# Mamba block and mixture of experts on one core: the skip of y and the output projection are issued half a step later, the kept columns are copied ahead of the first tap

## Chip, cores and metric

The kernel runs on one core of a Trainium2 chip, as one program and one launch. The time is device time in microseconds (us), lower is better. The engines are TensorE (PE for its matmuls, PEld for its weight loads), VectorE (DVE), ScalarE (ACT), GpSimd (POOL) and SyncE (SP, which issues most DMAs). Each has one queue and works it off in order.

## The reference, cut to what matters

Four sequences of 1024 tokens with 256 channels go through a Mamba block, a layer norm, a mixture of experts (MoE) and a second layer norm. All arithmetic is in float32.

```
h = x * rsqrt(mean(x*x) + 1e-5) * norm_scale
xs, res = split(h @ w_in)                       # 512 channels each
res = silu(res)
xs = silu(causal_depthwise_conv(xs, 4 taps) + conv_b)
delta, B, C = split(xs @ w_xproj)               # 16, 16 and 16 columns
delta = softplus(delta @ w_dt + b_dt)
state[t] = exp(delta[t] * A) * state[t-1] + (delta[t] * xs[t]) * B[t]   # 16 states a channel
y[t] = sum over states of state[t] * C[t]
out = (y + xs * D) * res                        # the skip is xs * D
x1 = layernorm(x + (x + out @ w_out))           # the sum of residuals: 2x + projection
normed = x1 * rsqrt(mean(x1*x1) + 1e-8) * norm_weight
moe = shared expert + 2 of 8 routed experts (256 -> 1024 -> 256, relu, sigmoid router)
result = layernorm(x1 + (x1 + moe))
```

## The kernel before, in words

**Tiling.** The tokens are cut into 8 chunks of 512: two for each of the four sequences. A tile of channels by tokens is 128 x 2048: four blocks of 128 channels, each with 512 tokens. The second chunk of a sequence needs the last three columns of the first (the halo of the convolution, kept in `halos`) and the last value of each state (kept in `state`).

**The scan loop.** The program's outer loop runs over 128 steps, 8 chunks by 16 states. One step of one state does:

- `over_partitions` (L427): PE spreads the row of B, and later that of C, over all partitions, into PSUM (`pb`).
- `inputs`: ACT copies `pb` to `b` (L439), DVE multiplies three blocks of `xs` by B (L441), POOL the fourth (L446). In the first chunk it is two and two.
- `scan`, for each block: ACT computes `da = exp(delta * A)` into PSUM (L454), of which two tiles exist, and DVE runs the recurrence along the tokens in place in `hs` (L457).
- `outputs`, half a step later: DVE multiplies `hs` by C (L470), POOL adds it to `y` (L471).
- `keep`: ACT copies the last column of the states (L465), in the first chunk of a sequence.

**Work beside the scan** is written as generators, which the loop advances by one `yield` each time it calls `side`. The list `beside` is advanced twice a step (behind the second and the fourth block), so one `yield` there is half a step. The list `ending`, used for the tail of the last chunk but one and of the last, is advanced after every block, a quarter of a step.

- `front(b, c)` prepares the next chunk: norm, projection, first tap of the convolution (ACT, L317) and its halo copy (ACT, L322), the other three taps (DVE, L325), the silus of `res` of the chunk before (L353) and of `xs` (L355), and softplus. There `y` serves as scratch up to `delta += y` (POOL, L411). Then the skip `y = D * xs` is made by four ACT instructions (L414), and `xs *= delta` by POOL (L417). For the first chunk, `alone` in the code, all of this lies ahead of the loop, on other engines in part.
- `tail(b, c)` finishes the chunk before: `y *= res` (POOL, L493), a wait, then in two halves the output projection `po` (PE, L503, 16 matmuls) and `summed = 2x + po` (DVE, L511) with its statistics; then the norm, the transposes for the router, its sigmoid (L568) and the routing (L575 and on), which feeds the MoE. The last chunk's tail multiplies on DVE and has no such wait.
- `moe` is a generator of its own, which `other_work` advances by 0.85 after every block: up (L841), relu on ACT (L850), down (L870), and gathers (SP) and scatters (POOL) of the routed rows. What is left of it runs after the scan.

The wait in the tail counts half steps, or quarters in the last two chunks:

```
def wait(halves, quarters):
    for _ in range(quarters if of in chunks[-2:] else halves):
        yield
```

**Order.** The program's order is not the engines' order: a scheduler moves instructions on each queue by its own estimate of when their inputs come. `tc.keep_in_program_order(ins)` pins an instruction behind the one that the program issued before it on the same engine. Before the change the pinned ones here are the first matmuls of the output projection and the scaling of `hn` in the front.

**Table loads.** ACT needs another table set for silu, for sigmoid, for the logarithm and for the exponential; the compiler puts a load (ACT_TABLE_LOAD) wherever the set changes in the order that the scheduler chose.

Of the kernel before, what the change touches and what calls it, by code (L numbers as in the profile page):

```python
# [10 lines left out]
ALU = mybir.AluOpType  # L11
# [7 lines left out]
K = 4  # L19
# [4 lines left out]
CHUNKS = [(512, 512)] * NSEQ  # L24
# [46 lines left out]
def mamba_moe_kernel(  # L71
# [18 lines left out]
    nc = tc.nc  # L90
# [92 lines left out]
    halos = const.tile([P, 2, KB, K - 1], F32, tag="halo", name="halos")  # L183
# [31 lines left out]
    def stats(src, mv, tiles, name):  # L215

        for t in range(tiles.start, tiles.stop):
            st = small.tile([P, 6], F32, tag="bnst", name=f"bnst_{name}_{t}")
            nc.vector.bn_stats(st, src[:, t, :])  # L219
            nc.vector.bn_aggr(mv[:, t, :], st)  # L220
# [40 lines left out]
    def front(b, c):  # L261
        s = f"{b}_{c}"
        TC, TT = LEN[b, c], LEN[b, c] // P
        x_sb = xs_in[b, c]


        alone = (b, c) == chunks[0]
# [22 lines left out]
        def projected(m):  # L290
            pi = ps_mix.tile([P, TC], F32, tag="mix", name=f"pi_{s}_{m}")
            for k in range(KD):
                nc.tensor.matmul(  # L293
                    pi, lhsT=w_in_sb[:, k, m * P : (m + 1) * P], rhs=hT[:, k, :],
                    start=(k == 0), stop=(k == KD - 1),
                )
            return pi
# [16 lines left out]
        for k in range(KB):  # L314
            pi, xk = projected(k), xs[:, k, :]
            yield
            nc.scalar.activation(  # L317
                xk, pi, AF.Identity,
                bias=chan_sb[:, k, CB : CB + 1], scale=chan_sb[:, k, CW + K - 1 : CW + K],
            )  # L320
            if c + 1 < len(CHUNKS[b]):
                nc.scalar.copy(halos[:, c % 2, k, :], pi[:, TC - (K - 1) :])  # L322
            for back in range(1, K):
                tap = chan_sb[:, k, CW + K - 1 - back : CW + K - back]
                nc.vector.scalar_tensor_tensor(  # L325
                    xk[:, back:], pi[:, 0 : TC - back], tap, xk[:, back:], ALU.mult, ALU.add
                )
            if alone:
                nc.scalar.activation(xk, xk, AF.Silu)
            yield  # L330
# [77 lines left out]
        for blocks in [slice(k, k + 1) for k in range(KB)] if alone else [slice(0, KB)]:  # L408
            db, xb = delta[:, blocks, :], xs[:, blocks, :]
            engine = nc.vector if alone else nc.gpsimd  # L410
            engine.tensor_tensor(db, db, y[:, blocks, :], ALU.add)  # L411
            yield
            for k in range(blocks.start, blocks.stop):
                nc.scalar.activation(  # L414
                    y[:, k, :], xs[:, k, :], AF.Identity, scale=chan_sb[:, k, CD : CD + 1]
                )
            engine.tensor_tensor(xb, xb, db, ALU.mult)  # L417
        scans[b, c] = (xs, delta, y, parts, gate)
        yield
# [54 lines left out]
    def turns(of):  # L474
# [5 lines that stand above are left out]
        return wait  # L480

    def tail(b, c):
        s = f"{b}_{c}"
        TC, TT = LEN[b, c], LEN[b, c] // P
        at = P + b * SEQ + FIRST[b, c]
        own_sums = sums_of[at : at + TC, :]
        wait = turns((b, c))
        x_sb, res, y = xs_in.pop((b, c)), gates.pop((b, c)), scans.pop((b, c))[2]
        if (b, c) == chunks[-1]:
            for k in range(KB):  # L490
                nc.vector.tensor_tensor(y[:, k, :], y[:, k, :], res[:, k, :], ALU.mult)
        else:
            nc.gpsimd.tensor_tensor(y, y, res, ALU.mult)  # L493
            yield from wait(3, 6)

        summed = two.tile([P, TT, D], F32, tag="rowset", name=f"summed_{s}")
        mv = small.tile([P, TT, 2], F32, tag="mv", name=f"mv_{s}")
        for half in range(2):
            po = ps_mix.tile([P, TT // 2, D], F32, tag="mix", name=f"po_{s}_{half}")
            for i in range(TT // 2):  # L500
                t = half * TT // 2 + i
                for k in range(KB):
                    ins = nc.tensor.matmul(  # L503
                        po[:, i, :], lhsT=y[:, k, t * P : (t + 1) * P], rhs=w_out_sb[:, k, :],
                        start=(k == 0), stop=(k == KB - 1),
                    )
                    if i == k == 0:
                        tc.keep_in_program_order(ins)
            yield from wait(1, 2)
            two_of = slice(half * TT // 2, (half + 1) * TT // 2)  # L510
            nc.vector.scalar_tensor_tensor(  # L511
                summed[:, two_of, :], x_sb[:, two_of, :], 2.0, po, ALU.mult, ALU.add
            )
            stats(summed, mv, two_of, s)
            yield from wait(1, 0)
# [504 lines left out]
    for _ in front(*chunks[0]):  # L1020
        pass
# [5 lines left out]
    for i, step in enumerate(order):  # L1027
        b, c, n = step
        place = chunks.index((b, c))
        more = i + 1 < len(order)  # L1030
        for k in range(KB):
            if k == 0 and more and n + 1 < N:
                over_b = over_partitions(order[i + 1], n + 1)
            if k == KB // 2:
                over_c = over_partitions(step, N + n)
                if more and n + 1 == N:
                    over_b = over_partitions(order[i + 1], 0)
            scan(step, hs, [k])
            if k == 0 and late is not None:
                keep(*late[0:2])  # L1040
            if k == KB // 2 - 1:
                if late is not None:
                    outputs(*late)
                    if n == 0:
                        list_of = ending if place + 1 == len(chunks) else beside
                        list_of.append(tail(*chunks[place - 1]))
                if n == 0 and place + 1 < len(chunks):
                    beside.append(front(*chunks[place + 1]))
                if n == 3:
                    beside.append(scans[b, c][4]())  # L1050
                if n == N // 2 and place + 2 < len(chunks):
                    xs_in[chunks[place + 2]] = load_x(*chunks[place + 2])
                side(beside)
            if k == KB - 1:
                late = (step, hs, over_c)
                if more:
                    hs = inputs(order[i + 1], over_b)
                side(beside)
            side(ending)
            other_work(LEN[b, c] / MAXC)  # L1060
    keep(*late[0:2])
    outputs(*late)
    ending.append(tail(*chunks[-1]))
    while ending:
        side(ending)
# [71 lines left out]
```

## Time and profile before

| | before |
|---|---|
| median of 3 runs | 1607.16 us (1602.42 to 1608.75) |
| the profiled execution | 1604.24 us |
| its span | 1602.5 us (1.74 outside it) |
| mean granted clock of TensorE | 0.881 |
| busy PE, DVE, ACT, POOL | 75%, 81%, 67%, 72% |
| table loads on ACT | 56 of 1283 ns |
| copy of one halo (L322) | 152 ns, 16 of them |
| one skip instruction (L414) | 707 ns, 32 of them |
| `delta += y` (L411) and `xs *= delta` (L417) on POOL | 4.5 to 4.7 us, 7 each |
| `y *= res` (L493) on POOL | 4.75 us, 7 |
| one half of the output projection (L503) | 5.5 us |
| `summed` (L511) | 0.67 us, 16 |

In the profile's groups and timeline an instruction is named by its line, engine and operation, then the output and inputs by the names of their tiles. A bracket at the end of a timeline line tells how long the engine stood idle ahead of the instruction, and what ended this. `x4` means that four instructions of a kind followed each other. Rows of waits give the waiting engine, tile and line, what released it, and then the total in us, the number and the longest. Windows give the busy time of PE, PEld, DVE, ACT and POOL with the number of instructions, then the clock, the share of the DMA engines and GB/s.

### The profile page before, as it was taken

Reading aid. Unit: us, or ns where it says so; the run is one execution under the profiler, and the core shown is the slowest. Engines: PE = TensorE matmul, PEld = TensorE weight load, DVE = VectorE, ACT = ScalarE, POOL = GpSimd, SP = SyncE. Lnnn points to the kernel's source line nnn. Section 1 sums busy time; section 2 is a strip of 40 time slices with the busy share of each in tenths; the row PEclk is TensorE's granted clock in tenths of the full one; section 3 lists DMA queues with packets and bytes.
Section 4 is the critical chain, followed back from the end, with each engine's and each line's share of the span. In section 5 each row is a group of like instructions: output and inputs, shape, how many; then the busy total and the mean of one; then the engine's idle time right before and its main releaser. Section 6 shows DMA issues by size and latency. Waiting matters only on the chain. (4 is left out here: it accounts for less than half of the span.)

```text
span 1602.5 us, 19985 instructions
## 1 busy us (share of the span) xinstructions
PE 1205.6 (75%) x6216; PEld 911.2 (57%) x6216; DVE 1294.8 (81%) x1435; ACT 1069.2 (67%) x2353; POOL 1157.8 (72%) x899
## 2 busy tenths in 40 slices
PE   5254156865678698878888888788878888899990
PEld 1111023653256576667566766675657767789990
DVE  4899899979998798989998999899989899420005
ACT  6556647875678677887688678866896766444442
POOL 2577986798669876898779977997699877531223
PEclk9575577988879999999989999899899999999995
DMA  5000000251016663366326642574176538659996
GB/s 146 0 0 0 0 13 14 83 145 43 14 40 181 181 181 82 123 202 187 82 70 200 213 109 67 169 214 115 44 210 177 160 82 255 188 154 324 312 279 217
DMA packets 160272, 211.59 MB, mean 132 GB/s; under 512 B 20617, under 2 KB 138130, under 8 KB 160162
## 3 DMA queue, kind: packets, MB, share of 16 engines
q1 hardware_dynamic: 135954, 181.75, 35.2%
q0 software_dynamic: 17216, 21.57, 7.5%
q10 hardware_dynamic: 6992, 6.95, 1.3%
q8 instruction: 51, 0.84, 0.2%
q14 instruction: 59, 0.48, 0.1%
HBM read 178.97 MB, written 31.27 MB: 131 GB/s over the span
## 5 line engine op out<-in xcount | busy, mean ns | idle before, releaser
L471 POOL TENSOR_TENSOR y<-y,hs 128x2048 f32<-128x2048 f32 x128 | 596.6, 4661 | 80.3 <-DVE hs L470 80.0
L454 ACT ACTIVATE da<-delta,chan_sb 128x512 f32<-128x512 f32 x512 | 353.0, 694 | 197.2 <-DVE hs L457 194.6
L870 PE MATMUL pd<-w,h 128*128 128x256 f32 x1600 | 386.2, 385 | 24.5 <-ACT h L850 11.6
L870 PEld LDWEIGHTS pd<-w,h 128*128 128x128 f32 x1600 | 298.3, 193 | 91.6 <-issue 20.4
L457 DVE TENSOR_TENSOR_SCAN hs<-da,state,hs 128x512 f32<-128x512 f32 x256 | 317.8, 1270 | 26.1 <-ACT da L454 24.9
L457 DVE TENSOR_TENSOR_SCAN hs<-da,hs 128x512 f32<-128x512 f32 x256 | 302.2, 1209 | 26.1 <-ACT da L454 25.5
L841 PEld LDWEIGHTS pu<-xT,w 128*128 128x128 f32 x2176 | 273.3, 201 | 62.7 <-ACT xT L824 43.8
L841 PE MATMUL pu<-xT,w 128*128 128x128 f32 x2176 | 278.0, 286 | 26.3 <-ACT xT L824 26.3
L470 DVE TENSOR_TENSOR hs<-hs,pb 128x2048 f32<-128x2048 f32 x128 | 290.8, 2272 | 3.0 <-PE pb L427 1.6
L850 ACT ACTIVATE h<-pu,wb 128x128 f32<-128x128 f32 x800 | 228.4, 367 | 69.0 <-PE pu L841 63.9
L446 POOL TENSOR_TENSOR hs<-xs,b 128x512 f32<-128x512 f32 x144 | 202.9, 1418 | 80.2 <-ACT b L439 59.6
L441 DVE TENSOR_TENSOR hs<-xs,pb 128x1536 f32<-128x1536 f32 (+1 forms) x128 | 213.6, 1669 | 14.2 <-ACT b L439 7.9
L427 PE MATMUL pb<-parts,pick 128*128 128x512 bf16 x256 | 106.5, 420 | 131.1 <-DVE hs L470 48.7
L903 POOL DMA_INDIRECT sums<-rb,xb x68 | 107.9, 1587 | 132.4 <-ACT xT L824 48.9
L293 PE MATMUL pi<-hT,w_in_sb 128*128 128x512 f32 x256 | 147.7, 707 | 43.5 <-DVE xs L325 17.2
L841 PEld LDWEIGHTS pu<-x1T,w 128*128 128x128 f32 x1024 | 131.8, 205 | 13.8 <-issue 10.4
L841 PE MATMUL pu<-x1T,w 128*128 128x128 f32 x1024 | 137.3, 291 | 0.0
L219 DVE BATCH_NORM_STATS2 bnst_l<-o 128x6 f32<-128x256 f32 x32 | 11.9, 410 | 152.3 <-DMA o<-sums 152.3
L293 PEld LDWEIGHTS pi<-hT,w_in_sb 128*128 128x128 f32 x256 | 51.4, 217 | 124.5 <-issue 37.9
L439 ACT COPY b<-pb 128x512 f32<-128x512 f32 x128 | 75.4, 589 | 28.1 <-PE pb L427 24.0
L503 PE MATMUL po<-w_out_sb,y 128*128 128x256 f32 x256 | 67.3, 423 | 31.4 <-POOL y L493 26.7
L427 PEld LDWEIGHTS <-pick 128*128 128x128 bf16 x256 | 26.5, 107 | 112.3 <-DVE hs L441 50.0
(188 smaller groups left out, 1380.3 us busy)
## 6 DMA issues: line engine op xcount, KB each, us to landing
w<-in_ew SPq DMA_DIRECT2D x136, 1024.0 KB, 5.9
w<-in_sw SPq DMA_DIRECT2D x16, 1024.0 KB, 5.5
xb<-rows SPq DMA_DIRECT2D x68, 129.0 KB, 5.0
x<-in_x SPq DMA_DIRECT2D x8, 512.0 KB, 4.3
sums<-summed ACTq DMA_DIRECT2D x8, 512.0 KB, 2.9
sums<-rs POOLq DMA_DIRECT2D x16, 256.0 KB, 6.0
o<-sums SPq DMA_DIRECT2D x3, 1024.0 KB, 9.1
out<-o ACTq DMA_DIRECT2D x3, 640.0 KB, 3.3
```

Source lines behind the costliest of these rows:

```text
L293: nc.tensor.matmul(pi, lhsT=w_in_sb[:, k, m * P : (m + 1) * P], rhs=hT[:, k, :], start=(k == 0), stop=(k == KD - 1),)
L427: nc.tensor.matmul(pb, lhsT=pick[:, row : row + 1].to_broadcast([P, P]), rhs=scans[b, c][3], start=True, stop=True,)
L441: nc.vector.tensor_tensor(hs[:, 0:on_pool, :], xs[:, 0:on_pool, :], pb.unsqueeze(1).to_broadcast([P, on_pool, TC]), ALU.mult,)
L446: nc.gpsimd.tensor_tensor(hs[:, k, :], xs[:, k, :], copy, ALU.mult)
L454: nc.scalar.activation(da, delta[:, k, :], AF.Exp, scale=chan_sb[:, k, CA + n : CA + n + 1])
L457: nc.vector.tensor_tensor_scan(hs[:, k, :], da, hs[:, k, :], 0.0 if c == 0 else state[:, k, n : n + 1], ALU.mult, ALU.add,)
L470: nc.vector.tensor_tensor(hs, hs, pb.unsqueeze(1).to_broadcast([P, KB, LEN[b, c]]), ALU.mult)
L471: nc.gpsimd.tensor_tensor(y, y, hs, ALU.add)
L841: nc.tensor.matmul(pu[:, i, :], lhsT=w[:, k, at : at + P], rhs=xT[:, k, :], start=(k == 0), stop=(k == KD - 1),)
L850: nc.scalar.activation(t[:, i, :], pu[:, i, :], AF.Relu, bias=wb[:, m : m + 1])
L870: nc.tensor.matmul(pd, lhsT=hidden[h][:, i, :], rhs=w[:, m, :], start=(m == 0), stop=(m == HB - 1 and e is None),)
L903: nc.gpsimd.indirect_dma_start(sums_of[:, :], bass.IndirectOffsetOnAxis(xb[:, TOKEN : TOKEN + 1].bitcast(U32), 0), rb, None, compute_op=AL ...
```

## The change

It has four parts. The halo copy is issued ahead of the first tap instead of behind it; both read the same PSUM tile `pi`. The skip gets one more `yield` ahead of it, so it and `xs *= delta` behind it are issued half a step later; the skip's instructions are pinned in program order, except in the first chunk. The tail waits one turn more between `y *= res` and the output projection (4 half steps for 3, or 7 quarters for 6), and so does all that follows in the tail. The 16 instructions of `summed` are pinned in program order on DVE.

```diff
@@ front: convolution
             yield
+            if c + 1 < len(CHUNKS[b]):
+                nc.scalar.copy(halos[:, c % 2, k, :], pi[:, TC - (K - 1) :])
             nc.scalar.activation(
                 xk, pi, AF.Identity,
                 bias=chan_sb[:, k, CB : CB + 1], scale=chan_sb[:, k, CW + K - 1 : CW + K],
             )
-            if c + 1 < len(CHUNKS[b]):
-                nc.scalar.copy(halos[:, c % 2, k, :], pi[:, TC - (K - 1) :])
@@ front: skip
             engine.tensor_tensor(db, db, y[:, blocks, :], ALU.add)
             yield
+            yield
             for k in range(blocks.start, blocks.stop):
-                nc.scalar.activation(
+                ins = nc.scalar.activation(
                     y[:, k, :], xs[:, k, :], AF.Identity, scale=chan_sb[:, k, CD : CD + 1]
                 )
+                if not alone:
+                    tc.keep_in_program_order(ins)
             engine.tensor_tensor(xb, xb, db, ALU.mult)
@@ tail
             nc.gpsimd.tensor_tensor(y, y, res, ALU.mult)
-            yield from wait(3, 6)
+            yield from wait(4, 7)
@@ tail: sum of residuals
-            nc.vector.scalar_tensor_tensor(
-                summed[:, two_of, :], x_sb[:, two_of, :], 2.0, po, ALU.mult, ALU.add
-            )
+            tc.keep_in_program_order(
+                nc.vector.scalar_tensor_tensor(
+                    summed[:, two_of, :], x_sb[:, two_of, :], 2.0, po, ALU.mult, ALU.add
+                )
+            )
```

## The prediction

> **What bounds the kernel now.** The page's busy row and its forty slices come first: VectorE (DVE) is the busiest engine up to slice 34, then almost empty, while PE fills the slices behind it.
>
> ```profile
> PE 1205.6 (75%) x6216; PEld 911.2 (57%) x6216; DVE 1294.8 (81%) x1435; ACT 1069.2 (67%) x2353; POOL 1157.8 (72%) x899
> ...
> DVE  4899899979998798989998999899989899420005
> ```
>
> Next, the windows per chunk split the span into a ramp (0 to 48 us), the scan (48 to 1373), the rest of the MoE (1373 to 1560, PE 180.1 of 187 busy) and the last normalization (42.5). Two rows of the windows:
>
> ```profile
> 200.00:373.00 173.00, 117.97 (x503) 78.10 (x503) 161.60 (x165) 117.23 (x229) 135.72 (x101) 0.82 0.23 68
> 373.00:541.00 168.00, 121.18 (x538) 83.02 (x537) 155.06 (x162) 119.38 (x248) 133.81 (x96) 0.85 0.28 81
> ```
>
> The third figure behind the length is DVE. Over the eight chunks it is 139.87 + 161.60 + 155.06 + 156.66 + 157.97 + 158.44 + 157.87 + 144.24 = 1231.7 of 1325 us: DVE bounds the scan, and 93.3 us of idle is all that reordering can give. The change removes no DVE work, so I went to DVE's waits, and in the timeline to the ones that the moved instructions cause.
>
> ```profile
> DVE hs L457 <- ACT da L454: 50.4, 24, 5.3
> ...
> DVE xs L325 <- ACT halos L322: 14.3, 5, 7.0
> DVE summed L511 <- PE po L503: 10.5, 3, 5.3
> ```
>
> Columns: total, number, longest. The first row is half of the idle. The timeline of ACT, POOL and DVE shows one such wait in the making:
>
> ```profile
> 339.41 4.50 POOL L411 TENSOR_TENSOR delta<-delta,y 128x2048 f32<-128x2048 f32 x1
> ...
> 343.94 2.56 ACT L414 ACTIVATE y<-xs,chan_sb 128x512 f32<-128x512 f32 x4 [3.49 <-POOL delta L411]
> ...
> 347.62 2.46 DVE L457 TENSOR_TENSOR_SCAN hs<-da,state,hs 128x512 f32<-128x512 f32 x2 [5.29 <-ACT da L454]
> ```
>
> ACT is in order. The skip (L414) waits 3.49 us for POOL's addition, runs 2.56, and the exponential that DVE wants stands behind it. So does the output projection, which waits for POOL's product (L493) and then makes DVE wait for `po`:
>
> ```profile
> 549.10 5.10 POOL L493 TENSOR_TENSOR y<-y,res 128x2048 f32<-128x2048 f32 x1
> ...
> 554.25 5.49 PE L503 MATMUL po<-w_out_sb,y 128*128 128x256 f32 x16 [7.96 <-POOL y L493]
> ...
> 559.79 0.69 DVE L511 SCALAR_TENSOR_TENSOR summed<-x,po 128x512 f32<-128x512 f32 x1 [5.31 <-PE po L503]
> ```
>
> **Halo copy first.** 16 copies of 0.152 us (group row L322) change places with 16 first taps, nothing is added. In the ramp the copy of block 2 stands behind a table load and two silus (20.63 to 22.98), and DVE waits 1.32 us for it at 23.16; now about 0.4 is left: −0.9 (bounds −1.3 to −0.5). In the scan the waits at a first tap are 1.09, 1.11 and 4.55, together 6.8. A tap still needs both the copy and the first tap, so I take 0, bounds −6.8 to 0.
>
> **Skip half a step later, tied.** A half step is 168/16/2 = 5.25 us. L414 is followed by a DVE gap at all seven joints of chunks: 3.55, 5.29, 2.12, 2.85, 2.23, 3.12, 2.23 = 21.4 us. In the order in which the built programs stand on ACT, `da` of the third block is now ahead of the skip; then comes one skip, the fourth `da`, and three skips (at the first joint three and one).
> - Joints 1→2, 3→4, 5→6: the third block's scan starts without a gap at 342.33 (347.62 − 5.29). The one skip runs 343.94 to 344.65, the fourth `da` ends at 345.3; the fourth scan began at 348.85 (347.62 and one scan of 1.23), so 3.45 is gained. At the other two, the same working ends before the third scan does: the whole 2.85 and 3.12. Sum −9.4. POOL's `xs*=delta` (L417) comes a half step later, but ended at 352.9, and the next chunk's B product reads it at 369.0: 16 us of cover.
> - Joints 0→1 and 2→3: POOL runs without a break from 179.6 to 195.5 and almost so from 518.99 to 537.0, and DVE waits for it there (1.38, 2.47). What the skip no longer costs is waited for on POOL: 0.
> - Joints 4→5 and 6→7: 2.23 saved, but on POOL a block of the B product (1.3 us) is now ahead of L417. It ended at 876.6, DVE read it at 879.28; it will end at 877.9, DVE wants it at 877.05. 0.9 comes back: −1.3 each, −2.6.
>
> Sum −12.0; bounds −21.4 (all gaps go) and 0 (each is replaced). The pin adds a wait with a queue behind it: on ACT the fourth `da`, on DVE its scan.
>
> **Tail half a step later, summed tied.** Seven tails start the projection a half step later, by which time L493 is long done; `summed` stands behind scans of about 2.4 us a pair. The 5.31 in chunk 3 goes: −5.3 (bounds −5.3 to 0). The 3.89 and 1.33 in the last tail stay, for it has no such wait. If a `po` were late now, the pinned `summed` would hold all scans behind it, up to 5.3 us a time. Everything behind it moves too: statistics, ACT's row scaling, router, the issue of the sums (ACT's queue), gathers (SP) and scatters (POOL). They feed MoE work that has the rest of the chunk, and behind the last scan PE has the same matmuls in both orders (480 up, 252 down): 0. The pins at the projection are as before.
>
> **What it adds.** The built program has 64 table loads for 56. In chunks 3 to 6 the router's sigmoid no longer stands beside the silus, so sets are loaded once more: 8 × 1.283 = 10.3 us of ACT. A burst in chunk 2:
>
> ```profile
> 433.16 1.28 ACT L353 ACT_TABLE_LOAD   x1
> 434.45 1.91 ACT L353 ACTIVATE res<-res 128x2048 f32<-128x2048 f32 x1
> ...
> 436.47 1.28 ACT L454 ACT_TABLE_LOAD   x1
> 437.76 0.69 ACT L454 ACTIVATE da<-delta,chan_sb 128x512 f32<-128x512 f32 x1
> ```
>
> DVE had a C product (2.26) and a B product to do and lost under 0.2 here; the double burst of chunk 3 (629.70 to 636.17) cost it 0.90 and went under the router's DVE work. So a load costs DVE between 0 and 1.283; I take half, +5.2 (0 to +10.3), as the bursts lose that common cover.
>
> The Trainium skill ("ScalarE: Activation LUTs", What ACT_TABLE_LOAD costs) speaks against this part: a switch of set is about 2.66 us, 1.28 of load and 1.38 of draining, and calls are to be batched by set. The row shows the load at its 1.28, but ACT's copy before it ended 0.02 us ahead of it, so no drain beside it. By that page the eight switches would be 21.3, half of it on DVE 10.7, and the forecast 5.5 us higher.
>
> **Sum.** −0.9 − 12.0 − 5.3 + 5.2 = −13.0 on the profiled 1604.24 (span 1602.5 and 1.74 outside it): 1591.2. The runs' median, 1607.16, is 2.9 above that execution, so I forecast 1594.
>
> **Rivals.**
> - *Taken back on ACT (same), 0.21.* Sigmoid and silu bursts fall on first taps, all loads count (+10.3), the odd joints give only half (−4.7), and the `po` wait becomes another (0): −0.9 − 4.7 − 2.6 + 10.3 = +2.1, 1609. For it: ACT is 67% busy and in order. Against: 1.3 us bursts were hidden so far.
> - *POOL too late at the joints (slower), 0.15.* If L417 really ends a whole half step later, DVE's first B product of the next chunk waits at 0→1, 2→3, 4→5, 6→7: 4 × 5.25 = 21.0 in place of −2.6. −0.9 − 9.4 − 5.3 + 5.2 + 21.0 = +10.6, 1618. It decides from 2.7 us of delay (879.28 − 876.6) at two of the joints, and from the first at the other two. The order on POOL moves only 1.3 us ahead of it, which speaks against.
> - *All gaps go, 0.10:* −0.9 − 21.4 − 5.3 − 6.8 = −34.4, 1573.
> - *The skip does not move:* excluded, the built order shows it behind the third `da`.
>
> **Numbers.** The forecast case has 0.54 and reaches 1584 to 1604 by the bounds of loads and joints. A measurement here tells about 0.5% (8 us) from no change: faster is below 1599.1, slower above 1615.2. Faster: 0.10 and 0.44 of the 0.54; same: 0.10 of it and 0.19 of the first rival; slower: 0.15 and 0.02. The range, 1578 to 1614, takes in the first rival and most of the way to the third; it leaves out the rest of that one and POOL's.
>
> **What would show it.** Right: DVE's `da` wait falls from 50.4 to near 40, gaps at 347.62, 695.41, 1027.30 under 2; no `po` wait in the scan; ACT_TABLE_LOAD x64. DVE's busy time as before, scan stage near 1312. Wrong: B product waiting for POOL's L417 at the even joints by over 3 us; first taps or `da` waiting in steps 5 to 9 of chunks 3 to 6 by more than 5 us in sum; or the stage behind the last scan longer than 187.

## The result and the profile after

The changed kernel takes 1614.35 us (median of 8 runs, 1609.12 to 1617.95) against 1606.14 us (8 runs, 1601.61 to 1612.78): a ratio of 1.0051, interval 1.0030 to 1.0072. It is slower by 8 us where 13 us less was forecast. The profiled execution of the changed kernel took 1609.12 us, the lowest of its eight, so the two traces differ by only 4.9 us of span (1602.5 to 1607.4).

The page first: busy times as before, ACT up by 8 us.

```profile
PE 1205.6 (75%) x6216; PEld 915.2 (57%) x6216; DVE 1292.3 (80%) x1435; ACT 1077.1 (67%) x2361; POOL 1158.7 (72%) x899
...
DVE  4899899989998998898999989899989899220005
```

The windows that answer to the two of before:

```profile
199.00:367.00 168.00, 114.04 (x486) 77.31 (x485) 158.10 (x163) 115.48 (x226) 131.32 (x98) 0.81 0.21 63
367.00:532.00 165.00, 114.86 (x510) 77.79 (x511) 155.31 (x163) 117.52 (x242) 132.50 (x98) 0.87 0.27 80
```

From the first scan instruction of one chunk to that of the next, chunks 1, 2 and 3 went from 172.3, 168.1 and 180.5 us to 168.3, 165.1 and 171.4, but chunks 4, 5 and 6 from 164.2, 167.9 and 164.1 to 170.2, 174.6 and 166.5. Over the whole scan, from the first scan instruction to the end of the last C product, DVE idles 91.1 us where it idled 92.8, and the scan is 4.3 us shorter (1319.5 for 1323.8). What follows it is 8.3 us longer (235.7 for 227.4), the ramp ahead of it 0.9. The waits of DVE in the trace after:

```profile
DVE hs L460 <- ACT da L457: 45.7, 33, 5.3
...
DVE xs L325 <- ACT xs L319: 16.4, 10, 7.8
DVE hs L460 <- POOL hs L449: 11.3, 6, 2.9
...
DVE summed L515 <- PE po L506: 6.1, 2, 4.8
```

The wait for `da` fell a little, from 50.4 to 45.7, but has 33 pieces for 24; 11.3 us of waits for POOL's block are new (0.2 before). The timeline at the first odd joint (1→2) shows what became of the skip: behind the third `da` comes one instruction, then the fourth `da`, then three, and DVE runs the third and fourth scan without a gap where it had waited 5.29 us:

```profile
344.82 0.76 ACT L457 ACTIVATE da<-delta,chan_sb 128x512 f32<-128x512 f32 x1
345.45 0.77 ACT L415 ACTIVATE y<-xs,chan_sb 128x512 f32<-128x512 f32 x1
346.06 0.74 ACT L457 ACTIVATE da<-delta,chan_sb 128x512 f32<-128x512 f32 x1
...
346.67 1.98 ACT L415 ACTIVATE y<-xs,chan_sb 128x512 f32<-128x512 f32 x3
```
```profile
346.76 2.45 DVE L460 TENSOR_TENSOR_SCAN hs<-da,state,hs 128x512 f32<-128x512 f32 x2
```

Earlier in the same queue stands the new loss of the scan:

```profile
328.31 0.37 ACT L891 COPY rs<-pd 128x256 f32<-128x256 f32 x1 [4.55 <-DMA sums<-rs]
...
332.06 0.69 ACT L390 ACTIVATE e<-pz,chan_sb 128x512 f32<-128x512 f32 x1 [2.85 <-PE pz L383]
...
333.74 0.69 ACT L457 ACTIVATE da<-delta,chan_sb 128x512 f32<-128x512 f32 x1
```
```profile
334.46 1.28 DVE L460 TENSOR_TENSOR_SCAN hs<-da,state,hs 128x512 f32<-128x512 f32 x1 [5.35 <-ACT da L457]
```

The first fence is ACT, the second DVE. `rs` collects two blocks of the shared expert and has one buffer, so ACT's copy of the next pair waits for the DMA of the pair before. Behind that copy on ACT stand the softplus instruction `e` and the `da` that DVE wants; PE waits too, for its one PSUM tile `pd` is not read out (19.3 us in all in the trace after), and `pz`, which `e` reads, is behind `pd`. The row of waits, of before and then of after:

```profile
ACT rs L886 <- DMA sums<-rs: 10.1, 3, 3.6
```
```profile
ACT rs L891 <- DMA sums<-rs: 36.7, 8, 5.5
```

The other loss is behind the scan. From the last spread row (L427, now L430) to the last matmul PE takes 207.0 us for 202.1, with 1278 matmuls either way, and what comes behind that matmul 40.8 for 39.3. The PE and POOL timelines of after show where it stops:

```profile
1419.46 0.41 PE L630 MATMUL pr<-sofar,ones 128*128 128x40 f32 x2 [3.41 <-POOL sofar L612]
```
```profile
1412.22 1.55 POOL L908 DMA_INDIRECT sums<-rb,xb  x1 [8.56 <-ACT h L855]
1416.78 1.55 POOL L908 DMA_INDIRECT sums<-rb,xb  x1 [3.01 <-issue]
1417.78 1.62 POOL L612 TENSOR_TENSOR sofar<-sofar,both 128x8 f32<-128x8 f32 x4
```

The counts of the last chunk's routing (`sofar`) are behind two scatters of the MoE on POOL, and PE waits for them at the head of its queue. In the trace of before the same four additions started at 1412.29.

### The profile page after: what moved, and what is told of

It reads as the page before. It is cut to its first block, busy times and chain, and to the rows that moved or that the text cites. A ratio compares the mean times of both kernels' runs of the same rounds, so it can differ in the third digit from the quotient of the medians.

```text
span 1607.4 us, 19973 instructions
## 1 busy us (share of the span) xinstructions
PE 1205.6 (75%) x6216; PEld 915.2 (57%) x6216; DVE 1292.3 (80%) x1435; ACT 1077.1 (67%) x2361; POOL 1158.7 (72%) x899
## 5 line engine op out<-in xcount | busy, mean ns | idle before, releaser
L474 POOL TENSOR_TENSOR y<-y,hs 128x2048 f32<-128x2048 f32 x128 | 604.9, 4726 | 84.3 <-DVE hs L473 84.2
L875 PE MATMUL pd<-w,h 128*128 128x256 f32 x1600 | 396.7, 395 | 37.4 <-ACT rs L891 19.3
L875 PEld LDWEIGHTS pd<-w,h 128*128 128x128 f32 x1600 | 307.9, 199 | 98.6 <-ACT rs L891 20.9
L846 PEld LDWEIGHTS pu<-xT,w 128*128 128x128 f32 x2176 | 266.8, 198 | 41.9 <-ACT xT L829 27.2
L846 PE MATMUL pu<-xT,w 128*128 128x128 f32 x2176 | 270.8, 282 | 9.7 <-ACT xT L829 9.6
L449 POOL TENSOR_TENSOR hs<-xs,b 128x512 f32<-128x512 f32 x144 | 200.6, 1420 | 47.4 <-ACT b L442 27.4
L430 PE MATMUL pb<-parts,pick 128*128 128x512 bf16 x256 | 107.5, 423 | 144.4 <-DVE hs L473 46.4
L846 PE MATMUL pu<-x1T,w 128*128 128x128 f32 x1024 | 141.6, 291 | 0.0
L430 PEld LDWEIGHTS <-pick 128*128 128x128 bf16 x256 | 26.1, 104 | 113.3 <-DVE hs L444 51.9
L325 DVE SCALAR_TENSOR_TENSOR xs<-pi,chan_sb,xs 128x511 f32<-128x511 f32 (+2 forms) x96 | 70.1, 736 | 17.2 <-ACT xs L319 16.4
```

The lines of the kernel that those rows point to most:

```text
L430: nc.tensor.matmul(pb, lhsT=pick[:, row : row + 1].to_broadcast([P, P]), rhs=scans[b, c][3], start=True, stop=True,)
L449: nc.gpsimd.tensor_tensor(hs[:, k, :], xs[:, k, :], copy, ALU.mult)
L474: nc.gpsimd.tensor_tensor(y, y, hs, ALU.add)
L846: nc.tensor.matmul(pu[:, i, :], lhsT=w[:, k, at : at + P], rhs=xT[:, k, :], start=(k == 0), stop=(k == KD - 1),)
L875: nc.tensor.matmul(pd, lhsT=hidden[h][:, i, :], rhs=w[:, m, :], start=(m == 0), stop=(m == HB - 1 and e is None),)
```

## The experiments

Theory T held that the later tail costs what the skip gains; theory S that any reordering re-deals the queues. Each ratio is to the kernel before, timed in the same rounds.

| kernel | median us | ratio, 95% interval |
|---|---|---|
| e1_halo | 1606.99 | 0.9995 (0.9983 to 1.0008) |
| e2_skip | 1601.31 | 0.9959 (0.9943 to 0.9975) |
| e3_tail | 1635.75 | 1.0170 (1.0152 to 1.0189) |
| e4_sum | 1608.68 | 1.0004 (0.9989 to 1.0018) |
| e5_no_tail | 1602.52 | 0.9962 (0.9943 to 0.9981) |
| e6_tail_sum | 1638.63 | 1.0168 (1.0137 to 1.0199) |
| e7_po_only | 1630.85 | 1.0141 (1.0110 to 1.0171) |
| e8_norm_only | 1633.65 | 1.0144 (1.0116 to 1.0172) |
| f1_all_rs2 | 1596.16 | 0.9925 (0.9901 to 0.9948) |
| f2_tail_rs2 | 1617.62 | 1.0065 (1.0043 to 1.0087) |
| f3_rs2 | 1597.41 | 0.9939 (0.9919 to 0.9960) |
| f4_no_tail_rs2 | 1595.23 | 0.9918 (0.9897 to 0.9938) |
| g1_all_last | 1604.75 | 0.9991 (0.9976 to 1.0005) |
| g2_all_rs2_last | 1587.21 | 0.9877 (0.9855 to 0.9900) |
| g3_slim | 1607.06 | 1.0001 (0.9981 to 1.0020) |

**The parts alone.** e1_halo is before with the first hunk of the change, e2_skip with the second, e3_tail with the third, e4_sum with the fourth.

```diff
 e1:  copy(halos, ...) moved ahead of the first tap
 e2:  + yield, and keep_in_program_order(ins) for the skip
 e3:  - yield from wait(3, 6)      + yield from wait(4, 7)
 e4:  + keep_in_program_order(...) for summed
```

> Only the halo copy ahead of the first tap. Theory T (the later tail costs what the skip gains): about -1 us, the ramp's second gap of the taps near 0.4 us as in the changed kernel; scan gaps as before. Theory S (any reordering re-deals ACT's queue and the matmuls behind the last scan, whichever part it is): the matmuls behind the last scan take 205 us or more in place of 202, and the whole is 0 to +5 us.

> Only the skip half a step later, pinned. Theory T: the seven gaps behind the skip fall from 21.4 us to about 5, table loads stay 56, the whole is -8 to -13 us. Theory S: those gaps go, but gaps of 3 to 5 us come in steps 12 and 13, where an exponential stands behind softplus instructions that wait for PE; the whole is -3 to +5 us.

> Only the tail's wait, 4 half steps for 3 and 7 quarters for 6. Theory T: this part alone is +8 to +15 us, with DVE gaps at first taps in steps 4 to 6 and the stage behind the last scan longer by 5 us. Theory S: -5 to +5 us, the 5.31 us wait for the projection gone.

> Only the sum of residuals pinned on DVE. Both theories: within 3 us of before, since the wait of 5.31 us for the projection in chunk 3 stays or moves; the matmuls behind the last scan as before.

Theory T was right about where the loss sits, not about its size: one line, the wait, is +1.7%, about 27 us, where 8 to 15 were expected; halo copy and pin cannot be told from nothing. The skip alone gains 0.41%, 6.6 us, less than the 8 to 13 that T expected of it. The four together sum to +20 us, the whole change is +8: the parts do not add, which comes back below. Why the skip gains so little, the trace of e2_skip tells. DVE's wait for `da` is 30.8 us (50.4 before), but its B product waits for POOL's additions to `y`:

```profile
DVE hs L460 <- ACT da L457: 30.8, 24, 4.6
...
DVE hs L444 <- POOL y L474: 18.0, 6, 4.5
```

In before that last row was 4.8. The POOL timeline of e2_skip at the joint 1→2, then DVE's:

```profile
350.91 5.00 POOL L420 TENSOR_TENSOR xs<-xs,delta 128x2048 f32<-128x2048 f32 x1
355.40 4.99 POOL L474 TENSOR_TENSOR y<-y,hs 128x2048 f32<-128x2048 f32 x1
...
364.11 5.13 POOL L474 TENSOR_TENSOR y<-y,hs 128x2048 f32<-128x2048 f32 x1
```
```profile
369.27 1.75 DVE L444 TENSOR_TENSOR hs<-xs,pb 128x1536 f32<-128x1536 f32 x1 [4.47 <-POOL y L474]
```

`xs*=delta` itself came early enough, but the additions behind it did not, and they free the buffers of `hs`: there are three, and DVE was ready for the next.

**Around the tail.** e5_no_tail is the changed kernel without the third hunk, e6_tail_sum the third and fourth together. e7_po_only and e8_norm_only split the later tail into its two halves:

```diff
 e7:  - yield from wait(3, 6)      + yield from wait(4, 7)    # ahead of the projection
      - yield from wait(3, 6)      + yield from wait(2, 5)    # behind rsqrt, ahead of the norm
 e8:  - yield from wait(3, 6)      + yield from wait(4, 7)    # behind rsqrt only
```

> The changed kernel with the tail's wait of before (3, 6); halo copy, later pinned skip and pinned sum stay. If the later tail is what costs: -5 to -9 us against before, as the skip alone (-0.41%). If the parts need each other (a pinned sum and a skip at the old place of the tail get into each other's way): 0 to +10.

> The tail's later wait with the pinned sum, nothing else. The later tail alone was +1.7%. If the pin only ties a short instruction: +24 to +30 us. If the pin is what makes the later tail cheaper in the whole change (the parts alone sum to about +20, the whole is +8): +10 to +18 us.

> The output projection and its sum half a step later, as in the tail part, but the wait ahead of the layer norm shortened by as much (2, 5 for 3, 6), so that norm, router, routing and the MoE stand where they were. If the projection's own place costs: +15 to +27 us as the tail part. If it is the later routing, which moves the MoE against the softplus on ACT and PE: within 5 us of before, and the waits of 5 us in step 12 are absent.

> The other half: projection and sum where they were, the wait ahead of the layer norm longer by half a step (4, 7). If the later routing costs: +15 to +27 us with waits over 5 us for the exponential in step 12 of chunks 1, 3 and 5, and more table loads. If the projection's place costs: within 5 us of before.

Without the later tail the change is a gain of 0.38%. The pin does nothing for a late tail: in e6 every engine has its instructions in the order of e3. e8 is the slow one that was expected of a later routing, with gaps of 5.62, 5.62 and 5.38 us in step 12 of chunks 1, 3 and 5 and 63 table loads. e7 missed both readings. Its step 12 is as in before and it has 56 loads, but it is slow in another way, for shortening the second wait was a change of its own: ACT now comes to the norm before POOL has its shift, and waits for it 14.8 us in all (3.6 in before). Its ACT line in chunk 7:

```profile
1271.82 1.09 ACT L243 ACTIVATE hn<-summed,shift_n,root_l 128x256 f32<-128x256 f32 x2 [5.83 <-POOL shift_n L240]
```

Whether these waits are all of its 1.4% is not shown, and e7 does not say what the projection's place alone is worth.

**Two buffers for rs.** The pool had no room, so `proj` and `combT` (16 and 9 partitions) share one tile, and `b2_sb` lies in the tile of `w_dt_sb`. DVE, ACT and POOL keep their order throughout; on PE a few small matmuls of `pz` and `pd` change places with their neighbours.

```diff
-  shared_rows[b, c] = one.tile([P, 2, D], F32, tag="rs", ...)
+  shared_rows[b, c] = two.tile([P, 2, D], F32, tag="rs", ...)
-  proj = one.tile([R, TC], ...)           + proj = shared_sb[0:R, 0:TC]
-  combT = one.tile([E + 1, TC], ...)      + combT = shared_sb[QUAD:, 0:TC]
```

f1 is this on the changed kernel, f2 on e3, f3 on before, f4 on e5; g3 is before with the moved tiles alone.

> The changed kernel with two buffers for the tile rs of the shared expert in place of one (room is made by laying two small tiles into partitions that others leave free); every queue keeps its order. Theory R: the later routing puts ACT's copy into rs, which waits for the DMA of the pair before (36.7 us in all against 10.1 in before), ahead of softplus and the exponentials, and that is the loss. Then the wait is near 0, the gaps of 5 us in step 12 of chunks 1 and 5 and those of 3 us for the state in step 13 of chunks 4 and 6 are gone, and the time is 15 to 25 us below the changed kernel's 1614. Rival P: the exponential waits behind softplus for PE, which is behind with the MoE for its own reasons: within 5 us of the changed kernel.

> Only the later tail, with two buffers for rs. Theory R: the later tail alone was +27 us; 15 to 22 of that are gone, +5 to +12 stays. Rival P: +22 to +30.

> The kernel before with two buffers for rs: the control. Theory R: it loses ACT's three waits of 3.6 us at most, of which one gap of 2.34 us on DVE in step 11 of chunk 1 is seen: -2 to -6 us. Rival P: within 2 us.

> Halo copy, later pinned skip and pinned sum with the tail of before (which was -0.38%) and two buffers for rs. Theory R: -8 to -13 us, the lowest so far. Rival P: as without the buffers, -6.

> The kernel before with only the two small tiles (the projected delta's input, and the routing weights with their bias) laid into other partitions, rs with one buffer: within 2 us of before if the gain of f3_rs2 (-9.8) is that of the buffers; -5 to -10 if it is that of the tiles.

Theory R holds where it matters: the changed kernel goes from 1.0051 to 0.9925, about 20 us, its scan is 15.9 us shorter (1303.6 for 1319.5), and ACT's wait for the DMA of `rs` (36.7) is gone from the rows. With the same order on DVE and ACT, the scan that had waited 5.35 us for its `da` starts without a gap. DVE of f1:

```profile
326.96 1.28 DVE L461 TENSOR_TENSOR_SCAN hs<-da,state,hs 128x512 f32<-128x512 f32 x1
```

The moved tiles are worth nothing (1.0001). The buffer also gains 0.6% on before, where 2 to 6 us were expected, and 0.44% on e5: the wait was there all along, and the later tail made it two to three times as dear. With two buffers the tail costs the change almost nothing (f4 to f1: 0.9918 to 0.9925, the intervals overlap), where it had cost 0.89% (e5 to the changed kernel). Without the later skip it stays dear: f2 is about 1.3% over f3, with gaps of 6.37, 6.59 and 6.56 us behind the skip in step 13 of chunks 1, 3 and 5 (6.10, 2.85 and 3.12 in f3). So the later skip is worth 6.6 us by itself and over 20 beside the later tail (e3 to the changed kernel, f2 to f1, halo copy and pin included), which is why the parts do not add. One side of this stands in the rows: the B product waits 18.0 us for POOL's additions with the skip moved alone and 15.5 with the tail alone, but 6.4 with both. And where `rs` has two buffers, skip, halo copy and pin without the later tail bring only 2 us (f3 to f4), not clear of noise.

**The stage behind the scan.** g1 is the changed kernel, g2 is f1, each with one line more:

```diff
         for k in range(KB):
             nc.vector.tensor_tensor(y[:, k, :], y[:, k, :], res[:, k, :], ALU.mult)
+        yield                                # last chunk only
```

> The changed kernel with one more turn ahead of the output projection of the last chunk, which puts the matmuls of the last routing back to where before has them among the MoE's. If their order behind the last scan costs the 5 us: the time from the last spread row to PE's end falls from 207 to near 202, PE's wait of 3.4 us for POOL's sums is gone, and the time is 3 to 6 us below the changed kernel's. If PE only lags for other reasons: no change within 2 us.

> Both cures together, two buffers for rs and the last tail one turn later. If both causes stand and add up: 1590 to 1594, the lowest of all, -0.9 to -1.1%. If the second is none: 1596 as with the buffers alone.

PE and POOL of g1, then the windows behind the last spread row, of after and of g1:

```profile
1412.85 0.31 PE L631 MATMUL pr<-sofar,ones 128*128 128x40 f32 x2
```
```profile
1410.07 1.05 POOL L613 TENSOR_TENSOR sofar<-sofar,both 128x8 f32<-128x8 f32 x4 [2.99 <-DVE both L588]
```
```profile
1360.00:1567.00 207.00, 195.29 (x1278) 179.55 (x1278) 26.25 (x61) 86.51 (x275) 60.61 (x60) 0.98 0.80 244
```
```profile
1359.00:1561.00 202.00, 192.77 (x1278) 177.33 (x1278) 26.47 (x61) 86.92 (x276) 60.92 (x60) 0.99 0.81 251
```

POOL's additions are ahead of the scatter again, PE does not wait, the same 1278 matmuls take 201.3 us (207.0), and all that is behind the scan 227.9 (235.7). The kernel gains 0.6% over the changed one (1.0051 to 0.9991), more than the 3 to 6 us expected. Both cures add up: g2 is the lowest of all, 1.2% under before and below the 1590 to 1594 expected, and beats both kernels.

## Why the prediction was wrong

- **The mechanism it looked at was right.** The gaps behind the skip at the seven joints fell from 21.4 to 3.9 us (2.95, 0, 0.34, 0, 0.28, 0, 0.28): 17.5 where 12 was forecast. The wait for `po` in the scan is gone. The halo copy was worth less than forecast: the ramp's gap of 1.32 became two of 0.60 and 0.39.
- **Where the forecast was missed.** It was −13.0 us, the traces differ by +4.9. The scan gave −4.3 for −12.1, what is behind it +8.3 for 0, the ramp +0.9 for −0.9. The first two come from the two steps below, which the prediction put at 0 in one sentence; the ramp takes 50.0 to 54.0 us in the traces here, so its share cannot be told from that spread.
- **The step that failed first:** "They feed MoE work that has the rest of the chunk ... : 0". I asked whether the MoE has time enough, not what it meets. Its instructions stand in ACT's and PE's in-order queues between softplus and `da`; half a step later the third block of the shared expert, with its wait for a DMA, falls ahead of `e` and `da`. That row, 10.1 us in before, was in the waits and I did not use it. It is 36.7 after, and taking it away is worth 20 us (f1).
- **The second:** "behind the last scan PE has the same matmuls in both orders". It is the same set, but not the same order: the projection, transposes and routing of the last chunk stand elsewhere among the MoE's. That cost 4.9 us up to the last matmul in the trace, and undoing it gained 9.6 by the medians (g1). Counting is no comparison of orders. That the last tail "has no such wait" was true and beside the point, since the MoE around it had moved.
- **The term for POOL at the joints** held in the changed kernel, where the B product waits 6.4 us for POOL's additions and 1.9 for `xs` (4.8 and 1.4 before), but not for the reason given. "16 us of cover" was reckoned to the reader of `xs`. What counts are the additions behind `xs*=delta`, which free `hs`: alone, the later skip turned 13.2 us (4.8 to 18.0) into waits for POOL and gained 6.6 us, not 12. That is the rival "POOL too late", at two thirds of its price and with the buffers of `hs` in place of `xs`; that the later tail takes most of it away again was no part of the reckoning.
- **The table loads,** weighed by half of 10.3, were not the loss. f1 keeps all 64 and is 1.3% faster than the changed kernel. f4 has 55; f1's scan, from first scan to last C product, is 7.5 us the shorter (1303.6 and 1311.2), and the two kernels' times cannot be told apart. What eight or nine loads cost by themselves no run shows, so the term of 5.2 stays open. Nor does a run show the 2.66 us that the Trainium skill ("ScalarE: Activation LUTs", What ACT_TABLE_LOAD costs) gives for a switch of set: the rows of a load have 1.28 us in every trace here, and in before ACT's instruction ahead of each but the first ended 0.02 us earlier.
- **The signs set out beforehand** worked in part. The three named gaps went, the `po` wait too, and 64 loads came, but the `da` wait is 45.7 where near 40 was set. Of the signs for being wrong, the longer stage behind the scan came (194.9 us for 188.1 from the last C product to the last matmul). First taps and `da` waited 10.7 us in steps 5 to 9 of chunks 3 to 6, over the 5 that were set; but they wait 6.1 there in before and 12.1 in f1, which is faster than before, so this sign told nothing. Step 12, which was not named, held the largest gaps (5.35 and 5.30).
- What stays open: why the skip at its old place makes the late tail so dear (f2 against f3), beyond the gaps that the trace shows there, and the projection's own place.

## What to carry to other kernels

When a step is moved, list every instruction that it releases later on each in-order queue, and ask of each what it can wait for and what will then stand behind it; an off-path wait on a single buffer becomes a wait of the critical engine as soon as the order shifts. Look for such a wait in the profile before tuning places: here a second buffer for a small tile gained 0.6% on the kernel before, the later skip 0.4%, and the two do not simply add. Compare the order, not the count, of what runs behind a long stage, above all where two engines feed each other.

## What was not expected of the hardware

PE's granted clock falls around its longer pauses behind the scan. In windows of 20 us after the change it was 0.92 and 0.91 in and behind a pause of 5.74 us (1360 to 1400), 1.00, 0.91 again behind one of 3.41 us (1420 to 1440), and 1.00 from there on; in before it was 0.91 only behind the pause of 4.44 us (1380 to 1400), and 1.00 around those of 2.41 and 1.90 us. The dips are short and deep: 0.57 from 1376 to 1384 and 0.72 from 1420 to 1426 after the change. A pause may so cost more than its length; no run prices that. And a tile of 256 KB, read by a DMA with 6.0 us from issue to landing (median of before), held ACT for up to 5.5 us at a time, which the list of busy engines does not show.
